# Two selective-scan layers in one kernel: channels regrouped from 128 + 64 into three blocks of 64

## The chip, the cores and the metric

The kernel runs on one core of a Trainium2 chip. The metric is the device time of one execution in microseconds. The kernel before took 1862.71 us (median of 3 runs, 1862.12 to 1892.24). Engine names are those of the profile: PE is TensorE (matmuls, PEld its weight loads), DVE VectorE, ACT ScalarE, POOL GpSimd, SP the engine that here only issues DMAs.

## The reference

Two layers follow each other on an image of 64 x 64 tokens with 96 channels. Each is `x = x + layer(groupnorm(x))`. Cut to what matters (the second layer; the first has raster scans along rows and columns in place of the snake):

```python
xin, z = split(x @ in_proj_w.T)              # 96 -> 192 + 192 channels
xc = silu(depthwise_conv3x3(xin))            # 192 channels
xs = [xc, reversed, snake order, reversed snake]          # 4 directions, 4096 tokens
x_dbl = xs @ x_proj; dts, B, C = x_dbl                     # 6, 16, 16 values a token
dt = softplus(dts @ dt_proj + bias)
h  = h * exp(dt * A) + dt * u * B            # along the tokens, 192 channels x 16 states
y  = sum over states (h * C) + u * D
y  = layernorm(sum of the 4 directions, put back) * silu(z)
out = y @ out_proj_w.T
```

The first layer computes its scan by cumulative sums with a decay in the divisor; past the first tokens of each direction the decay has underflowed and nothing is added.

## The kernel before

**Layout.** Channels lie on the 128 partitions, tokens along the free dimension. Channels 0 to 127 are in `u0` (scan input) and `y0` (result), both [128, 4096]. Channels 128 to 191 are in `ud` [128, 4096], which holds them twice, in the lower and the upper 64 partitions (the copy is made by DMA), and in `y1` [128, 2048], where the two partition halves hold different half-chunks of tokens.

**Stages**, in order, for each of the two layers: `head` (groupnorm, input projection, conv, silu, gate to DRAM), the scans, and `tail` (layernorm, gate, output projection, residual).

- `head(l)` projects in eight steps of 512 tokens, copies the result by ACT into padded images `pad0`, `pad1`, and runs six convolutions `conv(b, c)` of [128, 1024]: nine taps each on DVE (L1011 for the first, L1013 for the others), silu on ACT. `y0 = u0 * D` is made by ACT (L1018) after each conv; `y1 = ud * D` by POOL in `start_y1` (L920 to L923), two instructions of 64 x 2048 at the end.
- Layer 0 scans only in `near_scans`: in each direction the first 192 tokens for the slowest states, fewer for the faster ones (`STAY`), in 8 units. A flag computed from the data says whether that is enough; it is in this input, so the full scan under `tc.If` is not executed, and all full scan tiles are layer 1's.
- Layer 1 runs `scans`: 16 groups (2 orders x 2 directions x 4 chunks of 1024 tokens), each with 24 tiles of [128, 1024]. The first 16 (T=0) are one state of channels 0 to 127; the other 8 (T=1) are two states of channels 128 to 191, one in each partition half. 384 tiles in all.
- `tail(l)` runs eight steps of 512 tokens, in a software pipeline of `centre` (mean by matmul with `pos`, subtraction, square), `scale` (variance by matmul, reciprocal root on ACT, gain and gate on DVE), `project` (output projection, residual add on DVE), and in layer 1 `tokens` (transposes and store).

**One scan tile.** PE spreads a row of B over the partitions into PSUM (L777, weights `sel` or `selh`), ACT makes `m = exp(dt * A)` into PSUM (L792), DVE makes `b = B * du` (L793) and scans `h = m * h + b` (L816), POOL multiplies by a spread row of C (L832; `cb` is loaded from DRAM by one DMA of 512 KB for T=0, two of 256 KB for T=1), and PE adds the tile to `y` in PSUM (L857): for T=0 with the identity, for T=1 with `fold`, which sums the two partition halves and gives 64 rows. The last state of a T is followed by a copy of `y` by ACT (L863). The next T begins with loading `y` back into PSUM by identity matmuls (L854). PSUM holds one `y` [128, 1024], one `B`, and two `m`.

**Order.** The loop over tiles writes the order of the instructions by hand. At tile j it issues the C load of tile j+2, the B matmul and the exp and `b` of j+1, the scan of j, the C product of j-1, and the reduction of j-5 (`LAG`). The prelude of the next group (projection of x to B, C and dt; splitting of B into three bf16 parts, L580; softplus) is cut into steps that are put between the tiles. Softplus is `delta(T)`: ACT L619 to L628 and POOL L629 (`w`), L632 (`ln`), L635 (`dt`) and L638 (`du`), on [128, 1024], once for each T. For the first group, all of it lies ahead of the first `b`.

Queues run in order. SP issues all loads and stores, so a DMA that waits for data holds up those behind it.

The weights of the scans are loaded by `scan_weights`, 26 small DMAs for each layer and order.

Of the kernel before, what the change touches and what calls it, by code (L numbers as in the profile page):

```python
# [16 lines left out]
HW = 64  # L17
L = HW * HW
DM = 96
DI = 192  # L20
NS = 16
RK = 6
TC = 1024
NCH = L // TC
NEAR = 3 * HW


STAY = ((NEAR, 0, 1, 0, 1), (96, 1, 2, 0, 0), (64, 2, 4, 1, 2), (32, 4, NS, 2, NS // 2))
# [7 lines left out]
NV = 16  # L36


@with_exitstack
def two_ss2d_layers(  # L40
# [11 lines left out]
):  # L52

# [31 lines left out]
    make_identity(nc, ident)  # L85
    pos = const.tile([128, 128], F32, name="pos")
    nc.vector.memset(pos, 1.0 / DI)
    fold = const.tile([128, 128], F32, name="fold")
    for h in range(2):
        nc.vector.tensor_add(fold[:, 64 * h : 64 * h + 64], ident[:, 0:64], ident[:, 64:128])  # L90
# [16 lines left out]
    sel = const.tile([NB, 32, 128], BF16, name="sel")  # L107
    nc.vector.tensor_copy(sel, i3.unsqueeze(2).to_broadcast([NB, 32, 128]))
# [8 lines left out]


# [6 lines left out]
    u0 = pers.tile([128, L], F32, name="u0")  # L125
    ud = pers.tile([128, L], F32, name="ud")
    y0 = pers.tile([128, L], F32, name="y0")

    y1 = pers.tile([128, L // 2], F32, name="y1")
    xs = dpool.tile([DM, L], F32, name="xs")  # L130

# [15 lines left out]
    def views(l, p, base, cc):  # L147


        n = base.shape[-1] // NCH  # L150
        if p == 0:
            return [(base[:, cc * n : (cc + 1) * n], lambda s: s)]
        if l == 0:
            v = base.rearrange("p (h w) -> p w h", w=HW)
            k = TC // HW
            return [
                (v[:, cc * k : (cc + 1) * k, :], lambda s: s.rearrange("p (w h) -> p w h", h=HW))
            ]

        k = n // HW // 2  # L160
        v = base.rearrange("p (r two w) -> p r two w", two=2, w=HW)[:, cc * k : (cc + 1) * k]

        def part(o):
            return lambda s: s.rearrange("p (r two w) -> p r two w", two=2, w=HW)[:, :, o, :]

        return [(v[:, :, 0, :], part(0)), (v[:, :, 1, ::-1], part(1))]

    def columns_of_half(base, h, cols):

        half = slice(64 * h, 64 * h + 64)  # L170
        v = base[half].rearrange("p (c r w) -> p w c r", c=NCH, w=HW)[:, cols]

        def part(s):
            return s[half].rearrange("p (w c h r) -> p w c h r", c=NCH, h=2, r=TC // HW // 2)[
                :, :, :, h, :
            ]

        return v, part

    def near_views_y1():  # L180

        k = NEAR // HW
        lo, hi = slice(0, 64), slice(64, 128)
        out = [
            (0, y1[lo, 0:NEAR], lambda s: s[lo]),
            (1, y1[hi, L // 2 - NEAR :][:, ::-1], lambda s: s[hi]),
        ]
        for h in range(2):
            v, part = columns_of_half(y1, h, slice(0, k))
            out.append((2, v, part))  # L190
            v, part = columns_of_half(y1, h, slice(HW - k, HW))

            out.append((3, v, lambda s, part=part: part(s[:, ::-1])))
        return out

    def near_views(base):

        v = base.rearrange("p (h w) -> p w h", w=HW)
        k = NEAR // HW

        def flat(s):
            return s

        def columns(s):
            return s.rearrange("p (w h) -> p w h", h=HW)

        return [
            (base[:, 0:NEAR], flat),
            (base[:, L - NEAR :][:, ::-1], flat),
            (v[:, 0:k, :], columns),  # L210
            (v[:, HW - k :, :][:, ::-1, ::-1], columns),
        ]
# [5 lines left out]
    def scan_weights(l):  # L218

        xw, dwb, am = [], [], []
        for p in range(2):
            lp = 2 * l + p
            w = swp.tile([128, 4, NC], F32, tag=f"xw{p}", name=f"xw{lp}")
            v = swp.tile([128, 4, 128], F32, tag=f"dwb{p}", name=f"dwb{lp}")
            e = swp.tile([128, 4, NS + 1], F32, tag=f"ab{p}", name=f"ab{lp}")
            a = swp.tile([128, 2, 4, NS], F32, tag=f"am{p}", name=f"am{lp}")
            nc.vector.memset(v[96:128], 0.0)
            for d in range(2):  # L230
                r = slice(NB + RK * d, NB + RK * d + RK)
                rr = slice(RK * d, RK * d + RK)
                hi = slice(64 * d, 64 * d + 64)
                c0 = NB + 2 * RK + NS * d
                for q, T in ((d, d), (2 + d, 2)):
                    nc.sync.dma_start(out=w[:, q, 0 : NC - NS], in_=xpw[lp, :, T, 0 : NC - NS])
                    nc.sync.dma_start(
                        out=w[:, q, NC - NS :], in_=xpw[lp, :, T, c0 : c0 + NS]
                    )
                nc.sync.dma_start(out=v[r, d, :], in_=dtw[lp, rr, d, :])  # L240
                nc.sync.dma_start(
                    out=v[NC : NC + 1, d, :],
                    in_=alb[lp, :, d, NS : NS + 1].rearrange("p o -> o p"),
                )
                nc.sync.dma_start(out=e[:, d, :], in_=alb[lp, :, d, :])
                for h in range(2):
                    half = slice(64 * h, 64 * h + 64)
                    nc.sync.dma_start(out=v[r, 2 + d, half], in_=dtw[lp, rr, 2, hi])
                    nc.sync.dma_start(
                        out=v[NC : NC + 1, 2 + d, half],  # L250
                        in_=alb[lp, hi, 2, NS : NS + 1].rearrange("p o -> o p"),
                    )
                    nc.sync.dma_start(out=e[half, 2 + d, :], in_=alb[lp, hi, 2, :])

            nc.scalar.activation(a[:, 0, 0:2], e[:, 0:2, 0:NS], AF.Exp)
            for h in range(2):
                half = slice(64 * h, 64 * h + 64)
                nc.scalar.activation(
                    a[half, 0, 2:4, 0 : NS // 2], e[half, 2:4, h:NS:2], AF.Exp
                )  # L260
            nc.vector.tensor_scalar_mul(a[:, 1, 0:2], a[:, 0, 0:2], -0.5)
            nc.vector.tensor_scalar_mul(
                a[:, 1, 2:4, 0 : NS // 2], a[:, 0, 2:4, 0 : NS // 2], -0.5
            )
            nc.vector.tensor_scalar_mul(a[:, 0, 0:2], a[:, 0, 0:2], -1.0)
            nc.vector.tensor_scalar_mul(
                a[:, 0, 2:4, 0 : NS // 2], a[:, 0, 2:4, 0 : NS // 2], -1.0
            )
            xw.append(w)
            dwb.append(v)  # L270
            am.append(a)
        return xw, dwb, am

    def near_scans(weights):
# [5 lines left out]
        with ExitStack() as sc:  # L280
# [5 lines left out]
            def spare(name):  # L286
                return pps.tile([128, 1024], F32, tag="m", name=name, bufs=2)

            def parts(t):
                return t.rearrange("p (d w) -> p d w", w=NEAR)  # L290
# [3 lines left out]
            us = []  # L294
            for T, u in enumerate((u0, ud)):
                t = once.tile([128, WN], F32, name=f"nus{T}")
                for i, (v, f) in enumerate(near_views(u)):
                    copy = (nc.gpsimd.tensor_copy, nc.vector.tensor_copy, nc.scalar.copy)[i % 3]
                    copy(f(parts(t)[:, i]), v)
                us.append(t)  # L300
            halves = [slice(0, WN // 2), slice(WN // 2, WN)]
            for h, s in enumerate(halves):
                ps = spare(f"npj{h}")[0:NC, 0 : WN // 2]
                nc.tensor.matmul(ps, xw[:, 0, :], us[0][:, s], start=True, stop=False)
                nc.tensor.matmul(ps, xw[0:64, 2, :], us[1][0:64, s], start=False, stop=True)
                (nc.scalar.copy, nc.vector.tensor_copy)[h](xd[0:NC, s], ps)


            C = {}
            for w in sorted({w for w, *_ in STAY}):  # L310
                C[w] = dram.tile([NS, 4 * w], F32, name=f"nC{w}")
                nc.sync.dma_start(
                    out=C[w].rearrange("n (d w) -> n d w", w=w),
                    in_=parts(xd[NC - NS : NC])[:, :, 0:w],
                )

# [10 lines left out]

            dt, du, S = (
                [once.tile([128, WN], F32, name=f"n{nm}{T}") for T in range(2)]
                for nm in ("dt", "du", "S")  # L330
            )

            def delta(T):
                for h, s in enumerate(halves):
                    ps = spare(f"npd{T}{h}")[:, 0 : WN // 2]
                    nc.tensor.matmul(
# [918 lines left out]
```

## Time and profile before

| | us |
|---|---|
| timed runs | 1862.71, 1862.12, 1892.24; median 1862.71 |
| profiled execution | 1858.14 (span 1856.3, mean TensorE clock 0.853) |
| load and groupnorm statistics | 0 to 24 |
| head of layer 0 | 24 to 99 |
| near scans of layer 0 | 99 to 175 |
| tail of layer 0 | 175 to 249 |
| head of layer 1 | 249 to 330 |
| gap before the first `b` | 330 to 363 |
| scans of layer 1 | 363 to 1783 |
| tail of layer 1 | 1783 to 1856 |

The stages are read from the timeline: where the first and the last instruction of each lie. Inside the scans the period of one tile is 3.60 us: `b`, then the scan, on DVE, with small gaps. The data moved are 231.91 MB, mostly C rows spread over the partitions:

```profile
cb<-C SPq DMA_DIRECT2D x256, 512.0 KB, 4.4
cb<-C SPq DMA_DIRECT2D x256, 256.0 KB, 4.1
```

The columns are destination and source, the issuing queue, the number of DMAs, the size of each, and the median time from issue to landing in us.

### The profile page before, as it was taken

What the parts mean: (1) busy time and instruction counts of PE and PEld (TensorE: products, weight loads), DVE (VectorE), ACT (ScalarE), POOL (GpSimd) and SP (SyncE); (2) the same over time, 40 slices, a digit from 0 to 9 for tenths busy, and PEclk for the clock granted to TensorE, in tenths of its full rate; (3) what the DMA queues carried; (4) which work ended last, traced back from release to release, by engine and by line L of the source; (5) the groups of instructions that cost most, each with busy time, mean ns of one, the idle gap of its engine ahead of it and who ended that gap; (6) DMA issues with size and microseconds to landing.
All of it is one profiled execution on the core that took longest, in us unless ns stands there. A gap on an engine that the chain in (4) does not pass through costs nothing.

```text
span 1856.3 us, 12455 instructions
## 1 busy us (share of the span) xinstructions
PE 1416.7 (76%) x3427; PEld 519.5 (28%) x3427; DVE 1626.8 (88%) x1162; ACT 948.8 (51%) x1321; POOL 1262.0 (68%) x569
## 2 busy tenths in 40 slices
PE   6446973487778797978787878787878878797788
PEld 3014220122223232323232323233232323242322
DVE  7975679289999999999999999999999999999956
ACT  3453653445555645555464545555555564645323
POOL 0252003378888878797979797978888888889720
PEclk8555787588898998989898989898989899898969
DMA  4321312134454444445353545444445444544451
GB/s 98 89 57 45 86 43 68 53 131 131 150 148 141 149 142 142 137 147 156 117 171 124 150 141 144 148 133 161 129 148 148 148 145 135 148 142 148 137 135 34
DMA packets 90640, 231.91 MB, mean 125 GB/s; under 512 B 29984, under 2 KB 31440, under 8 KB 90464
## 3 DMA queue, kind: packets, MB, share of 16 engines
q1 hardware_dynamic: 88448, 230.23, 41.2%
q10 hardware_dynamic: 2112, 0.79, 0.2%
q8 instruction: 29, 0.48, 0.1%
q14 instruction: 51, 0.42, 0.1%
HBM read 216.72 MB, written 12.16 MB: 123 GB/s over the span
## 4 chain that ended last, share of the span: by engine, by line
DVE 49%; PE 14%; ACT 11%; POOL 9%; issue 4%; DVEq 1%; POOLq 0%; ACTq 0%
DVE h L816 36%; ACT m L792 9%; DVE b L793 9%; POOL hc L832 4%; PE y L857 4%; DVE acc L1013 3%; PE y L854 2%; PE B L777 2%; POOL w L629 1%; POOL dt L635 1%; POOL du L638 1%; PE v L1088 1%; PE pd L605 1%; DVEq L816 1%; PE m L1077 1%
## 5 line engine op out<-in xcount | busy, mean ns | idle before, releaser
L832 POOL TENSOR_TENSOR hc<-h,cb 128x1024 f32<-128x1024 f32 x384 | 896.6, 2358 | 230.8 <-PE y L857 138.3
L816 DVE TENSOR_TENSOR_SCAN h<-m,carry,b 128x1024 f32<-128x1024 f32 x288 | 676.7, 2350 | 43.6 <-ACT m L792 6.0
L792 ACT ACTIVATE m<-dt,am 128x1024 f32<-128x1024 f32 x384 | 427.8, 1115 | 392.2 <-DVE h L816 374.7
L793 DVE TENSOR_TENSOR b<-B,du 128x1024 f32<-128x1024 f32 x384 | 461.5, 1202 | 62.5 <-POOL du L638 33.3
L857 PE MATMUL y<-hc,ident 128*128 128x512 f32 x1024 | 507.7, 618 | 6.1 <-POOL hc L832 6.1
L777 PE MATMUL B<-B,sel 96*128 96x512 bf16 x512 | 168.0, 412 | 179.4 <-DVE b L793 178.7
L857 PEld LDWEIGHTS y<-hc,ident 128*128 128x128 f32 x1024 | 198.0, 197 | 217.5 <-issue 156.3
L816 DVE TENSOR_TENSOR_SCAN h<-m,b 128x1024 f32<-128x1024 f32 x96 | 219.9, 2290 | 15.4 <-ACT m L792 2.6
L857 PE MATMUL y<-hc,fold 128*64 128x512 f32 x512 | 181.1, 665 | 20.4 <-POOL hc L832 20.4
L826 ACT COPY carry<-h 128x1 f32<-128x1 f32 x288 | 52.9, 184 | 184.4 <-DVE h L816 183.8
L777 PEld LDWEIGHTS <-sel 96*128 96x128 bf16 x512 | 47.2, 100 | 356.4 <-issue 353.7
L777 PE MATMUL B<-B,selh 96*128 96x512 bf16 x256 | 79.1, 391 | 77.9 <-DVE b L793 77.9
L1013 DVE SCALAR_TENSOR_TENSOR acc<-pad,v,acc 128x1024 f32<-128x1024 f32 x96 | 130.3, 1418 | 0.3
L923 POOL TENSOR_SCALAR y<-ud,ds 64x2048 f32<-64x2048 f32 x4 | 38.7, 9671 | 127.2 <-DMA ud<-ud 127.0
L580 PE MATMUL rs<-xd,ident 96*96 96x512 f32 x128 | 69.1, 622 | 33.0 <-issue 32.0
L854 PE MATMUL y<-y,ident 128*128 128x256 f32 (+1 forms) x144 | 87.8, 768 | 6.0 <-ACT y L863 5.8
L629 POOL TENSOR_TENSOR w<-w,t 128x1024 f32<-128x1024 f32 x32 | 75.4, 2355 | 23.7 <-ACT t L628 23.7
L632 POOL TENSOR_TENSOR ln<-ln,w 128x1024 f32<-128x1024 f32 x32 | 75.2, 2349 | 2.4
L635 POOL TENSOR_TENSOR dt<-dt,ln 128x1024 f32<-128x1024 f32 x32 | 75.4, 2357 | 1.4
L857 PEld LDWEIGHTS y<-hc,fold 128*64 128x64 f32 x512 | 40.7, 147 | 126.5 <-issue 64.9
L605 PE MATMUL pd<-xd,dwb 29*128 29x512 f32 x128 | 70.1, 655 | 5.2 <-DVE h L816 5.2
L777 PEld LDWEIGHTS <-selh 96*128 96x128 bf16 x256 | 23.8, 99 | 179.3 <-issue 179.2
(185 smaller groups left out, 1385.3 us busy)
## 6 DMA issues: line engine op xcount, KB each, us to landing
cb<-C SPq DMA_DIRECT2D x256, 512.0 KB, 4.4
cb<-C SPq DMA_DIRECT2D x256, 256.0 KB, 4.1
szd<-sz SPq DMA_DIRECT2D x16, 256.0 KB, 2.2
szt<-szd SPq DMA_DIRECT2D x16, 256.0 KB, 5.3
xT<-xs SPq DMA_DIRECT2D x16, 192.0 KB, 5.4
szd<-sz SPq DMA_DIRECT2D x16, 128.0 KB, 2.2
ud<-ud SPq DMA_DIRECT2D x8, 256.0 KB, 3.1
szt<-szd SPq DMA_DIRECT2D x16, 128.0 KB, 5.7
```

The source lines that it names most:

```text
L605: nc.tensor.matmul(ps[:, s.start - o : s.stop - o], dwb[p][96 : NC + 1, 2 * T + d, :], xd[96 : NC + 1, s], start=True, stop=True,)
L629: nc.gpsimd.tensor_sub(w, w, t)
L632: nc.gpsimd.tensor_add(ln, ln, w)
L635: nc.gpsimd.tensor_add(dt[:, s], dt[:, s], ln)
L777: nc.tensor.matmul(ps[:, s.start - B0 : s.stop - B0], lhs, me["B3"][:, s.start - XB : s.stop - XB], start=True, stop=True,)
L792: nc.scalar.activation(a, me["dt", T], AF.Exp, scale=am[p][:, 0, q, n : n + 1])
L793: nc.vector.tensor_mul(b[:, rest], ps[:, XB - B0 : TC - B0], me["du", T][:, rest])
L816: nc.vector.tensor_tensor_scan(along(d, h), along(d, a), along(d, b), 0.0 if c == first else carry[T][:, n : n + 1], ALU.mult, ALU.add,)
L832: nc.gpsimd.tensor_mul(hc, live.pop(("h", j)), live.pop(("C", j)))
L854: nc.tensor.matmul(to, ident, of, start=(q == 0), stop=False)
L857: nc.tensor.matmul(ps[half] if split else ps[:, s], lhs[:, 0:64] if split else lhs, v[:, s], start=(n == 0 and not l), stop=(n == ns - 1),)
L1013: nc.vector.scalar_tensor_tensor(acc, src, wk, acc, ALU.mult, ALU.add)
```

## The change

All 192 channels become three blocks T = 0, 1, 2 of 64. `u[T]` and `y[T]` are [128, 2048]: the lower 64 partitions hold the first half of each 1024-token chunk, the upper ones the second half (`HALF`, `HT` = 512). Every scan tile is now 64 channels x two states; a group still has 24 tiles (3 blocks x 8 pairs of states) of [128, 1024]. The tile's own instructions on ACT, DVE and POOL keep their sizes.

- *Softplus* runs on [128, 512] for each of three blocks, half the columns; then `both` copies the result by DMA into the two-state layout, four DMAs of 128 KB each for `dt` and for `du`.
- *Reduction*: always `fold` into 64 rows, two column halves into one [128, 512] bank of `y`, two buffers. `y` is loaded back by one or two matmuls.
- *Projection* to B, C and dt: six matmuls over 64 rows at one step instead of two steps.
- *C rows*: always two DMAs of 256 KB.
- *Conv*: over whole padded rows, 2 x 526 contiguous elements instead of 16 x 64; the rows at the edges of the half-chunks come from extra matmuls (`borders`); `start_y` on POOL runs after each conv on 128 x 1024, six times per layer.
- *Near scans*: `u` gathered by PE, softplus once on [128, 1152], doubled by DMA, six units instead of eight.
- *Tail*: four steps of 1024 tokens, last chunk first, `pos` with a block for each half, output projection by six matmuls over 64 rows.
- *Scan weights*: 44 DMAs instead of 26 for each layer and order. The full scan of layer 0, not executed here, becomes a function of its own (`far_scans`).

The core of the diff:

```diff
-STAY = ((NEAR, 0, 1, 0, 1), (96, 1, 2, 0, 0), (64, 2, 4, 1, 2), (32, 4, NS, 2, NS // 2))
+FEWER = ((64, 1, 2), (32, 2, NP))
...
-    u0 = pers.tile([128, L], F32, name="u0")
-    ud = pers.tile([128, L], F32, name="ud")
-    y0 = pers.tile([128, L], F32, name="y0")
-    y1 = pers.tile([128, L // 2], F32, name="y1")
+    u = [pers.tile([128, L // 2], F32, name=f"u{T}") for T in range(3)]
+    y = [pers.tile([128, L // 2], F32, name=f"y{T}") for T in range(3)]
...
 (scans)
+                def project():
+                    ps = spare(f"pj{k}")[0:NC]
+                    for T in range(3):
+                        for h, half in enumerate(HALF):
+                            nc.tensor.matmul(
+                                ps[:, halves[h]], xw[p][half, d, T, :], me["u"][T][half],
+                                start=(T == 0), stop=(T == 2),
+                            )
...
+                    def lost():
+                        nc.gpsimd.tensor_sub(me["w"], me["w"], me["t"])
+                        nc.gpsimd.tensor_add(me["ln"], me["ln"], me["w"])
+                    def whole():
+                        nc.gpsimd.tensor_add(me["sp"], me["sp"], me["ln"])
+                        nc.gpsimd.tensor_mul(me["su"], me["sp"], me["u"][T])
+                    def double():
+                        for nm, of in (("dt", "sp"), ("du", "su")):
+                            t = me[nm, T] = pre.tile([128, TC], F32, tag=f"{nm}{T}", ...)
+                            both(t.rearrange("p (h t) -> p h t", h=2), me[of])
...
+                        (6, 7, 9, 10, 12, 13, 14, 15, 16, 17, 18, 19, 20, 21, 22),
+                        [
+                            copies, project, rows, lambda: residual(0), lambda: residual(1),
+                            *delta(0), *delta(1),
+                        ],
+                return early, list(enumerate(delta(2)))
...
-                    live["y"] = pps.tile([128, TC], F32, tag="y", name=f"y{l}_{j}")
+                    live["y"] = pps.tile([128, HT], F32, tag="y", name=f"ys{j}", bufs=2)
...
+                for h, half in enumerate(HALF):
+                    nc.tensor.matmul(
+                        ps[half], fold[:, 0:64], v[:, halves[h]], start=False, stop=(m == NP - 1)
+                    )
...
 (head)
+            def conv(b, s):
+                W2 = HW + 2
+                room = cw.tile([128, 2, SR, W2], F32, tag="acc", name=f"acc{l}_{b}_{s}")
+                acc = room.rearrange("p c r w -> p c (r w)")[:, :, 0 : SR * W2 - 2]
...
+                start_y(nc.gpsimd.tensor_scalar_mul, ds, b, cut)
+            for b in range(3):
+                project(b, 0)
+                project(b, 1)
+                borders(b)
...
 (tail)
+                for T in range(3):
+                    nc.tensor.matmul(pm, pos, y[T][:, cut], start=(T == 0), stop=(T == 2))
...
+                for T in range(3):
+                    for h, half in enumerate(HALF):
+                        nc.tensor.matmul(
+                            po[:, h], op[half, T, :], gs[T][half], start=(T == 0), stop=(T == 2)
+                        )
```

## The prediction

> **What bounds it now.** I read the busy line first, then the slices, the chain of waits, and the waits of VectorE inside the scan stage.
>
> ```profile
> PE 1416.7 (76%) x3427; PEld 519.5 (28%) x3427; DVE 1626.8 (88%) x1162; ACT 948.8 (51%) x1321; POOL 1262.0 (68%) x569
> ...
> DVE  7975679289999999999999999999999999999956
> ...
> DVE 49%; PE 14%; ACT 11%; POOL 9%; issue 4%; DVEq 1%; POOLq 0%; ACTq 0%
> ```
>
> VectorE (DVE) is at nine tenths from slice 10 to 38 and lower outside. So there are two regimes. The timeline gives these stages, in us from the span's start: load 0-24, head(0) 24-99, near scans 99-175, tail(0) 175-249, head(1) 249-330, a gap of 33 until the first `b`, the scans 363-1783 (1418.6 from first `b` to last scan) and tail(1) to the end. In the scan stage a tile costs one `b` and one scan:
>
> ```profile
> L816 DVE TENSOR_TENSOR_SCAN h<-m,carry,b 128x1024 f32<-128x1024 f32 x288 | 676.7, 2350 | 43.6 <-ACT m L792 6.0
> ...
> L793 DVE TENSOR_TENSOR b<-B,du 128x1024 f32<-128x1024 f32 x384 | 461.5, 1202 | 62.5 <-POOL du L638 33.3
> ...
> L857 PE MATMUL y<-hc,ident 128*128 128x512 f32 x1024 | 507.7, 618 | 6.1 <-POOL hc L832 6.1
> ```
>
> With the small gaps between instructions the timeline shows a cadence of 3.60 us (3.54 where the scan starts from a constant). 288 x 3.60 + 96 x 3.54 = 1377, so about 42 of the 1418.6 are waits. The waits of VectorE between 363 and 1783 name them (sum, number, mean):
>
> ```profile
> DVE b L793 <- PE B L777: 29.0, 36, 4.5
> DVE h L816 <- ACT m L792: 8.6, 11, 1.1
> ```
>
> (29.0 over 36 is 0.8 each; the last column is the largest.) The change keeps 384 tiles of 128x1024, so **the stage can give at most those 42 us**. The rest must come from the stages at both ends, here by windows (length; busy PE, PEld, DVE, ACT, POOL; TensorE clock; DMA share; GB/s):
>
> ```profile
> 24.00:99.00 75.00, 42.68 (x64) 12.41 (x64) 72.36 (x71) 37.42 (x55) 17.23 (x2) 0.64 0.26 65
> 99.00:175.00 76.00, 41.36 (x139) 26.59 (x139) 49.61 (x85) 41.09 (x82) 27.89 (x32) 0.52 0.17 36
> 175.00:249.00 74.00, 65.08 (x98) 17.14 (x98) 45.64 (x75) 40.22 (x48) 0.82 (x8) 0.75 0.36 93
> 249.00:330.00 81.00, 41.48 (x80) 14.18 (x79) 73.35 (x67) 34.52 (x50) 20.77 (x2) 0.73 0.19 52
> ```
>
> The heads are VectorE's (72 of 75, 73 of 81), the tails TensorE's (65 of 74), and near is bound by none.
>
> **What the Trainium skill says.** "SBUF — State Buffer", section "Who interferes with whom": a VectorE instruction with two SBUF inputs and GpSimd exclude each other on a shared port; one SBUF input does not. The trace agrees: a conv tap (L1013, pad and acc from SBUF) takes 1.28 us, but 4.62 and 4.64 us for the two that coincide with L923 on GpSimd; `b` (one input in PSUM) keeps 1.20 us beside `hc`. "TensorEngine Tiling (Array Packing)", section "Key Properties": matmuls in different rows or columns of the array run side by side. The trace agrees for columns: four `fold` records of 64 columns take 1.08 us, four `ident` records 1.9. For rows it shows two chance pairs only (`o` and `m` of the tail near 1810.6, 0.67 and 0.69 us, overlapping). "TensorE: Matmul & The Clock Gate" says an idle TensorE drops to half clock; in the trace 64x512 and 128x512 records cost 1.0 us in the first 24-29 us of a tail and 0.52 later.
>
> **The change, part by part** (estimates; plus is slower).
>
> *Scans.* Per tile: `exp`, `b`, scan and `hc` unchanged. TensorE: `ident` reductions (1.9 us) become `fold` pairs (1.1), so 256 tiles lose 0.8 us of TensorE; B matmuls are the same. The starting value of y is 1 or 2 `ident` matmuls of [128,512] for each T instead of up to 4, and y has two PSUM buffers, so that the next T does not wait for ACT's copy (L863). Those T switches are where B comes late: clock dips to 0.55 and most of the 36 waits lie there. GpSimd: 8 softplus operations of 2.35 us (18.8 per group) become 12 of 128x512. No row of that size is here; half of 2.35 is 1.18, so 14.1, bounds 12 and 18. ACT: 12 softplus activations of 1.1 become 18 of about 0.6 (half the columns above the 0.2 us that a small copy takes), less 2 us per group.
> Added: doubling `dt` and `du` by 8 DMAs of 128 KB for each T and group, 384 in all, 50 MB on 231.9 MB, and 8 x 0.45 = 3.6 us of SP's issue. They wait for GpSimd's `whole`, and queued behind them on SP are the `cb` loads; for these GpSimd's `hc` waits. A `cb` load is issued 10.8 us (three cadences) ahead of its `hc` and lands in 4.4, leaving 6.4; 3.6 of issue leaves 2.8. And `hc` may be late by a tile before the 4 `h` buffers stop VectorE. So I cost it at 0, bound 0 to +1 per burst, 48 in all. `dt(k+1, T)` itself is ready over five cadences ahead for T=0. C is now always two loads of 256 KB, 256 more issues on SP over 1377 us, same bytes: 0.
> What remains of the 42: about 14 (the first tiles, `exp` after a long ACT step). **-28, bounds -38 to +10.**
>
> *Start-up of the scans (33 us).* Six ACT softplus steps of 1.02-1.15 become 0.6 (-3), four GpSimd steps of 2.35 become 1.2 (-4.6), `y0` on ACT goes (-1.1), the doubling DMA adds 8 issues and one landing, 5.5 (`cb` of 256 KB: 4.1). **-4, bounds -8 to +4.**
>
> *Heads.* (a) Conv(0,0) now needs 9 in-projections and border matmuls ahead of it; before, it began 6.3-6.8 us after the first `xn`, behind pairs of 1.02-2.07 us. In-projection is cut from 16 full to 12 pairs of 64 columns, but border copies add 0.21 each: **+3.5** (+1 to +8). (b) A tap runs over 2 x 526 = 1052 elements instead of 1024: 54 taps x 1.2 x 2.7% = +1.7. (c) `ds*u`:
>
> ```profile
> L923 POOL TENSOR_SCALAR y<-ud,ds 64x2048 f32<-64x2048 f32 x4 | 38.7, 9671 | 127.2 <-DMA ud<-ud 127.0
> ```
>
> two of 9.67 us per layer, at the end of the conv become six of 128x1024 (about 4.8 each) after each conv, five of them under taps. Each stretched tap cost 4.63 - 1.28 = 3.35 us, twice: 6.7 per layer. A half as long operation should hold a tap half as long: 5 x 1.7 = 8.5, **+2**. ACT's `y0` goes, off the path. **+7 for each head** (+2 to +13).
>
> *Near.* ACT exp and tanh (24 + 24) and VectorE's three rows (6.4, 6.3, 11.6) come down by a quarter (6 units for 8), but `us` go through TensorE and ACT, softplus runs on the whole 1152 columns once, and 12 doubling DMAs put two landings of 3-4 us in the chain: -5 and +10. **+5** (-3 to +12).
>
> *Tails.* Per 1024 tokens `m` and `v` take 6 records each in place of 8 (block-diagonal `pos`), `o` 12 records of 64 rows that can go as 6 pairs in place of 8. The steady period is TensorE's: 6.27 us per 512 tokens, 2.1 + 2.1 + 2.06. New per 1024: 3.1 + 3.1 + 3.1 = 9.4 to 12.5 without row pairs, before 12.5. With four periods and fewer, longer steps: tail(0) 4 x 3.1 = **-12** (-16 to -2), tail(1), where the token transposes stay, **-10** (-14 to -2).
>
> *Setup:* `sel` cast of 2.3 us goes, `wide`, `fold2` come: **-1.5.**
>
> Sum: -28 - 4 + 14 + 5 - 22 - 1.5 = **-36**. The profiled execution took 1858.1 us (span 1856.3), so 1822; the median of the three runs, 1862.7, is 4.6 above, so 1826.5. I say 1826.
>
> **Rivals.**
> A. *The waits stay* (chance 0.17): VectorE bounds the scan stage by its own work, the waits move to another place (`exp` on ACT, whose queue holds three softplus blocks), and row pairs do not overlap in the tails. Then scans -8, tails -10 and the rest as above (-4, +14, +5, -1.5): -4.5, 1858. For it: 1.20 + 2.35 is untouched. Against it: the waits lie at the T switches, which the change removes.
> B. *Slower: SP's queue becomes the pacer* (0.16). Each doubling waits on SP for GpSimd, and `cb` behind it is late. It decides when the wait plus 3.6 us of issue plus 1 MB of transfer (3.2 us at 310 GB/s, which is 145 GB/s over the share 0.47) exceeds the 6.4 us of lead plus the tile that the `h` buffers hold (3.6), 10.0. If it does by 1.5 us in each of 48 bursts, +72 takes the place of -28: 1926; by 1.0 us, 1902. For it: a wait of one tile (3.6), 3.6 and 3.2 one after another make 10.4. Against: transfers begin while later ones are issued. Likewise the row projection, now in one step (12 records of 0.52): one after another they are 6.3 us before B(j+1) can follow, against 2.4 of cover.
> C. *Better* (0.19): the heads' start and GpSimd's multiplies hide (+2 each in place of +7), near gains its 5, the scan stage 36 of its 42: 1826 - 10 - 8 - 8 = 1800.
> The change does what it says: block sizes are in the code, so no case for that.
>
> **How the numbers follow.** My case (0.48) is 1826, its own range 1812 to 1842 from the parts' bounds, not all of them at one end. Leaving out most of B (over 1870) and the end of C (under 1795) gives 1795 to 1870. About 2% of the median, 1825.5 and 1900, is what a measurement of this kernel can tell from no change. Faster by over 2%: half of mine (0.24) and C (0.19): 0.43. Slower by over 2%: three quarters of B, 0.12. Same: half of mine, A, the rest of B, 0.45.
>
> **What would show it.** Scans: VectorE's waits on B fall under 10 us in sum, the cadence stays 3.60, first `b` to last scan about 1391; B (the rival) would show `hc` waiting for `cb`, and VectorE for `hc`. Tails: `m`, `v`, `o` at some 9.4 us per 1024 tokens, `o` records in overlapping pairs. Heads: conv starts 3.5 us later after `xn`, taps of 1.32 us, five stretched ones per layer. The first `b` comes 29 us after the end of the head's conv. I am wrong first if VectorE's cadence changes, or if the taps beside GpSimd are stretched more than in proportion to its length.

## The result: 16.9% slower, and the profile after

The changed kernel took 2175.23 us (median of 4 runs, 2174.01 to 2176.87) against 1862.41 for the kernel before: ratio 1.169, 95% interval 1.1665 to 1.1711. One of the four runs of before was in a slower state of the chip (1892.24 us) and is left out of the ratio. The busy line and three rows of the slices of the changed kernel's page:

```profile
PE 1418.6 (65%) x3694; PEld 369.2 (17%) x3694; DVE 1605.4 (74%) x1108; ACT 881.7 (41%) x1386; POOL 1266.7 (58%) x647
...
DVE  7845793867676868686868777777777777777795
...
POOL 0741086575656565656657575757575657574760
PEclk8556866757585858585767776766767676767558
```

VectorE's busy time is about the same as before (1605 for 1627 us) but it is spread over a span 319 us longer: no engine works more than 5 us longer, all wait more. The loss lies in slices 8 to 38. By the timeline, in us:

| stage | before | after | change | forecast |
|---|---|---|---|---|
| head of layer 0, to the end of its conv | 99 | 101 | +2 | +7, setup -1.5 |
| near scans | 75 | 94 | +19 | +5 |
| tail of layer 0 | 74 | 50 | -24 | -12 |
| head of layer 1 | 81 | 79 | -2 | +7 |
| gap, from the head's last tap to the first `b` | 34 | 33 | -1 | -4 |
| scans, first `b` to last scan | 1418.6 | 1766.8 | +348 | -28 |
| tail of layer 1 | 73 | 51 | -22 | -10 |

Outside the scans the change gains some 29 us (408.2 for 437.7; the rows are rounded), where the forecast had 8.5. The whole loss is in the scans. VectorE's waits there, beside the 29.0 and 8.6 us of before (sum, number of times, longest):

```profile
DVE h L815 <- POOL hc L824: 285.8, 76, 7.9
DVE b L806 <- PE B L793: 87.7, 91, 2.6
```

The scan waits for an `h` buffer, which GpSimd's (POOL's) `hc` frees. Why is `hc` late? POOL's own waits in the same stage:

```profile
POOL w L751 <- ACT t L748: 427.4, 46, 11.6
POOL hc L824 <- DVE h L815: 181.9, 109, 3.4
POOL hc L824 <- DMA cb<-C: 22.6, 17, 2.4
```

POOL is 58% busy and yet late: 427 us, 9.3 at a time, go into one instruction, the softplus subtraction `w`, which waits for ACT's last activation `t`. Waiting for C rows (`cb`) cost POOL only 22.6 us. One such place in the timeline of the changed kernel (start, length, engine and line, operation, tiles; in brackets the idle time before and who ended it), first POOL, then ACT:

```profile
1078.77 2.35 POOL L824 TENSOR_TENSOR hc<-h,cb 128x1024 f32<-128x1024 f32 x1 [3.26 <-DVE h L815]
1092.72 1.27 POOL L751 TENSOR_TENSOR w<-w,t 128x512 f32<-128x512 f32 x1 [11.60 <-ACT t L748]
1094.07 1.26 POOL L752 TENSOR_TENSOR ln<-ln,w 128x512 f32<-128x512 f32 x1
1095.42 1.26 POOL L755 TENSOR_TENSOR sp<-sp,ln 128x512 f32<-128x512 f32 x1
1096.76 1.26 POOL L756 TENSOR_TENSOR su<-sp,u 128x512 f32<-128x512 f32 x1
1097.97 9.27 POOL L824 TENSOR_TENSOR hc<-h,cb 128x1024 f32<-128x1024 f32 x4
```

```profile
1086.72 1.12 ACT L802 ACTIVATE m<-dt,am 128x1024 f32<-128x1024 f32 x1
...
1087.85 0.64 ACT L745 ACTIVATE w<-w 128x512 f32<-128x512 f32 x1
1088.38 1.11 ACT L802 ACTIVATE m<-dt,am 128x1024 f32<-128x1024 f32 x1
...
1090.03 0.71 ACT L747 ACTIVATE t<-w,one 128x512 f32<-128x512 f32 x1
...
1090.88 1.12 ACT L802 ACTIVATE m<-dt,am 128x1024 f32<-128x1024 f32 x1
1091.94 0.70 ACT L748 ACTIVATE t<-t,less 128x512 f32<-128x512 f32 x1
```

POOL stands still from 1081.1 to 1092.7 with three finished scans behind `w`, then does four `hc` in a row. ACT cannot reach `t` sooner: in its queue three `exp` (`m`) and carries stand before it, and those wait for the scans. The two queues disagree on where softplus belongs.

This order is not the one written in the loop. A planner orders each engine's instructions when the program is built. The disagreement can be counted in the built program: the number of `exp` that ACT issues before a `t`, less the number of `hc` that POOL issues before the `w` that reads it.

| kernel | lead at each softplus, in tiles |
|---|---|
| before | 1 |
| after | 5, 5, 6 |

(The first group, whose softplus lies ahead of the scans, is left out; the traces show the same leads.) With a lead of 1, `w` falls into its place: in the kernel before, it does not wait at all past the first group. In the changed kernel a `w` waits 9.4 us on average at a lead of 5 and 9.7 at 6. The waits are not in proportion to the lead; what a smaller lead costs, the experiments show.

### The profile page after: what moved, and what is told of

Same layout as the page of the kernel before. It is cut to its first block, busy times and chain, and to the rows that moved or that the text cites. A ratio compares the mean times of both kernels' runs of the same rounds, so it can differ in the third digit from the quotient of the medians.

```text
span 2175.0 us, 14719 instructions
## 1 busy us (share of the span) xinstructions
PE 1418.6 (65%) x3694; PEld 369.2 (17%) x3694; DVE 1605.4 (74%) x1108; ACT 881.7 (41%) x1386; POOL 1266.7 (58%) x647
## 5 line engine op out<-in xcount | busy, mean ns | idle before, releaser
L840 PE MATMUL ys<-hc,fold 128*64 128x512 f32 x1536 | 637.8, 871 | 205.5 <-POOL hc L824 204.7
L793 PE MATMUL B<-B,selh 96*128 96x512 bf16 x768 | 318.2, 508 | 311.2 <-DVE b L806 310.6
L751 POOL TENSOR_TENSOR w<-w,t 128x512 f32<-128x512 f32 x48 | 60.8, 1267 | 435.3 <-ACT t L748 435.3
L840 PEld LDWEIGHTS ys<-hc,fold 128*64 128x64 f32 x1536 | 109.4, 176 | 501.4 <-POOL hc L824 316.0
L883 POOL TENSOR_SCALAR y<-u,ds 128x1024 f32<-128x1024 f32 x12 | 98.8, 8246 | 86.7 <-ACT u L981 86.7
L979 DVE SCALAR_TENSOR_TENSOR acc<-pad,v,acc 128x1052 f32<-128x1052 f32 x96 | 121.8, 1334 | 0.3
L835 PE MATMUL ys<-y,ident 128*128 128x256 f32 (+1 forms) x144 | 87.6, 717 | 50.1 <-POOL y L883 37.8
L724 PE MATMUL pd<-xd,dwb 29*64 29x512 f32 x192 | 69.9, 815 | 18.2 <-ACT B L715 12.3
L752 POOL TENSOR_TENSOR ln<-ln,w 128x512 f32<-128x512 f32 x48 | 60.7, 1264 | 3.7
L755 POOL TENSOR_TENSOR sp<-sp,ln 128x512 f32<-128x512 f32 x48 | 60.7, 1266 | 1.3
```

Of the source, the lines that this page charges most:

```text
L724: nc.tensor.matmul(ps[half], dwb[p][96 : NC + 1, d, T, half], xd[96 : NC + 1, halves[h]], start=True, stop=True,)
L751: nc.gpsimd.tensor_sub(me["w"], me["w"], me["t"])
L793: nc.tensor.matmul(ps[:, s], pick(GROUPS[k][1], m), state[k]["B3"][:, s], start=True, stop=True)
L835: nc.tensor.matmul(f(live["y"]), ident, view, start=(q == 0), stop=False)
L840: nc.tensor.matmul(ps[half], fold[:, 0:64], v[:, halves[h]], start=False, stop=(m == NP - 1))
L883: mul(y[T][:, s], u[T][:, s], ds[:, T : T + 1])
```

## The experiments

Three theories. ORDER: POOL's queue is held by `w`. DOUBLING: the copies of `dt` and `du` hold up SP and the loads. CLOCK: TensorE, at a mean clock of 0.69 in place of 0.85, makes B late. (Line numbers of the edited kernels are up to five above those of the changed one.)

**POOL in the written order.**

```diff
+            sc.enter_context(tc.manual_schedule(engines={mybir.EngineType.Pool}))
             load_exp_ln()
```

> Edit: inside the scans of layer 1 GpSimd (POOL) issues its instructions in the written order; the other engines keep the planner's. Count of leads (exps that ACT issues ahead of the softplus' last activation t, less the hc products that POOL issues ahead of the subtraction w that reads t): 5 to 6 in the changed kernel, 1 in the kernel before, 1 to 3 here. Theory ORDER (POOL's queue is held by w, issued three to four tiles too early): POOL's wait on t falls from 435 us to about 48 x 1 tile x 3.6 = 170 or less, DVE's wait on hc from 286 to under 60, time 1850 to 1930. Theory DOUBLING (the 384 copies on SP and their 50 MB delay cb or du): the order of POOL changes nothing of it, time over 2100. Theory CLOCK (TensorE at 0.69 makes B late): over 2100.

1881.23 us (1880.59 to 1881.87; ratio 1.010 to before). One engine's order takes back 294 of the 313 us. VectorE's wait on `hc` is gone from the list; POOL's waits (sum, number, longest) show 62 us on `t`:

```profile
POOL hc L825 <- DVE h L816: 236.1, 148, 3.9
POOL w L752 <- ACT t L749: 61.9, 31, 4.5
```

ORDER holds: in the scans POOL issues only softplus and `hc`, so the place of softplus is all that this changes there by itself. But the clock stayed at 0.74, and VectorE still waits 82 us for B.

**POOL and ACT in the written order; all engines in it** (the same line with more engines, or none named).

> Edit: in the scans POOL and ACT both issue in the written order; lead 1 at every softplus, as in the kernel before. Theory ORDER: POOL's wait on t under 50 us, DVE's wait on hc under 20, first b to last scan about 1400, time 1830 to 1850; the TensorE clock returns to about 0.85 without being touched. Theory DOUBLING or CLOCK: over 2100.

1903.03 us, 22 more, although the lead is 1 everywhere: a miss. The written order puts four activations of softplus between two `exp`; VectorE waits 54 us for `exp` (18 in pool_written), and POOL still 110 for `t`.

> Edit: in the scans all engines and SP issue in the written order. Theory ORDER: within 20 us of the run with POOL and ACT in the written order, 1820 to 1860, since only those two queues were wrong. Theory DOUBLING: over 2100, or longer still, since the copies then sit on SP exactly between the cb loads.

1934.90 us, also a miss. VectorE's wait on B is 158 us. So the written order isn't good as such. The part of it that was needed is POOL's, the place of softplus.

Nor is a lead of 1 what counts. Over all the runs here, leads of 4 to 6 (the changed kernel, no_doubling, after_zero) go with 203 to 286 us of VectorE's waits on `hc`; with leads of 1 to 3 (all the others, the kernel before among them) VectorE waits on POOL for 1.1 us at most after the first `b`. A `w` with a lead of 3 does wait, 3.6 us on average in pool_written, but that stays on POOL. That the four `h` buffers take it up fits, and is not shown by a run of its own.

**Without the doubling**, in the changed kernel and with POOL in the written order.

```diff
                     def double():
+                        if k:
+                            me["dt", T], me["du", T] = state[0]["dt", T], state[0]["du", T]
+                            return
                         for nm, of in (("dt", "sp"), ("du", "su")):
```

> Edit: the copies of dt and du into the two-state layout are made for the first group only and used for all groups, so the result is that of other dt and du; softplus and everything else still run. 360 of 384 copies and 47 MB are gone. Theory ORDER: POOL's wait on t stays at some 400 us, time 2100 to 2180. Theory DOUBLING: 1840 to 1900.

2058.63 us: between the two theories. The planner answers to the missing copies with other orders (leads 5, 5, 4 in place of 5, 5, 6), so the run changes two things, and its 117 us can't be divided between them.

> Edit: POOL in the written order, and dt and du doubled by DMA in the first group only and used in all groups, so the result is that of other dt and du. If the doubling is hidden, as the prediction has it: 1870 to 1885, within 10 us of pool_written. If the copies hold up cb or B: 1830 to 1860.

1861.59 us (1855.45 to 1871.91), 20 below pool_written. At this point the doubling seemed to cost something. (The leads changed here too, from 3, 2, 1 to 2, 2, 2.)

**One zero matmul per tile.** In pool_written the TensorE timeline shows the same records at two speeds:

```profile
904.27 0.59 PE L794 MATMUL B<-B,selh 96*128 96x512 bf16 x2 [0.93 <-DVE b L807]
904.79 1.08 PE L841 MATMUL ys<-hc,fold 128*64 128x512 f32 x4
907.85 0.59 PE L794 MATMUL B<-B,selh 96*128 96x512 bf16 x2 [1.98 <-DVE b L807]
...
915.37 1.01 PE L794 MATMUL B<-B,selh 96*128 96x512 bf16 x2 [1.32 <-DVE b L807]
916.32 1.98 PE L841 MATMUL ys<-hc,fold 128*64 128x512 f32 x4
```

After gaps of 1 to 2 us per tile, B takes 1.01 for 0.59 us and the four records of a tile's `fold` pair 1.98 for 1.08: about half clock (granted 0.51 from 915 to 934 us). The edit, on top of POOL's written order, adds work that changes nothing in the result:

```diff
                 ps = live["y"]
+                nc.tensor.matmul(ps, zero, v[:, halves[0]], start=False, stop=False)
                 for h, half in enumerate(HALF):
```

> Edit: POOL in the written order as in pool_written (1881 us), and one extra matmul per tile with a weight matrix of zeros, added into the same y, so the result is unchanged and TensorE has about 0.95 us more work per tile. Theory IDLE CLOCK (the new fold reductions leave TensorE idle for some 2 us per tile, its clock is halved, and B comes late): the clock between 400 and 1780 us rises from 0.76 to 0.88 or more, VectorE's wait on B falls from 82 us to under 45, time 1835 to 1855. Theory LOAD (B is late because TensorE has too much queued at the prelude's steps): the wait on B grows to 100 or more, time 1890 to 1920.

1849.37 us (1847.13 to 1853.68), 32 less than pool_written; ratio to before 0.9932 [0.9924, 0.9939]. More work on TensorE made it faster. One window of pool_written, then the same one of pool_zero (length; busy PE, PEld, DVE, ACT, POOL; clock; DMA share; GB/s):

```profile
800.00:1000.00 200.00, 154.12 (x402) 34.18 (x401) 180.98 (x105) 101.02 (x164) 156.71 (x82) 0.75 0.74 175
```

```profile
800.00:1000.00 200.00, 167.08 (x517) 49.97 (x518) 185.66 (x108) 101.80 (x163) 160.44 (x83) 0.98 0.76 180
```

VectorE's waits on B in the two runs (sum, number, longest):

```profile
DVE b L807 <- PE B L794: 82.4, 93, 2.6
```

```profile
DVE b L809 <- PE B L796: 56.3, 49, 2.1
```

The clock rises from 0.75 to 0.98. VectorE's wait on B fell to 56, not below 45. IDLE CLOCK holds for the clock and the time; the planner's orders may have moved with the added matmul, which ys_first_no_zero below settles.

> Edit: the changed kernel with the planner's order on all engines, and only the zero matmul added. Leads of ACT over POOL 4 to 6, nearly as in the changed kernel (5 to 6). Theory ORDER FIRST (POOL's stall is most of the loss, the clock a smaller part of its own): the clock rises to 0.85 or more, time 2080 to 2160. Theory CLOCK FIRST (the half clock makes POOL's stall): 1850 to 1950.

2126.02 us, with the clock in the scans at 0.88 to 0.91: 49 of the 313 us come back while POOL's leads stay high (4, 5, 6). ORDER comes first.

**The weights of layer 1 later** (a try at the near scans).

```diff
+                i = nc.scalar.activation(a[half, 0], e[half, :, :, h:NS:2], AF.Exp)
+                if l:
+                    tc.keep_in_program_order(i)
...
-        sw = scan_weights(l)
+        sw = None if l else scan_weights(l)
         head(l, xT, w)
+        sw = sw or scan_weights(l)
```

> Edit: POOL in the written order, and layer 1's scan weights are loaded and their exponentials issued on ACT after the head of layer 1, so that they stand in no queue during the near scans. Theory WEIGHTS (the near scans are longer by some 18 us mainly because ACT and VectorE wait 11 us for these loads): near falls from 94 to about 83, time 1868 to 1873. Theory CHAIN (the near scans' length is their own chain, doubling DMAs and TensorE at half clock): near 90 to 94, time 1877 to 1885.

1878.32 us (1875.69 to 1882.76), 3 less: CHAIN, not WEIGHTS. VectorE waits as long in the same place (11.6 us for 11.0), now for ACT's copy of the projection.

> Edit: both of these on top of the written order on POOL. If IDLE CLOCK and WEIGHTS hold, their gains add: 1825 to 1845, below the kernel before. If only one holds: 1845 to 1870.

1848.66 us (1846.60 to 1852.08): no gain on pool_zero.

**VectorE too in the written order.**

> Edit: as pool_zero (POOL in the written order, one zero matmul per tile; 1849 us), and VectorE too issues in the written order. On VectorE the planner has put two scans and then two b one after another at 30 places in the changed kernel and in pool_zero, at 15 in pool_no_doubling, at none in layer 1 of the kernel before, and here at one. There is one B buffer, so the second b of such a pair must wait for its B. Theory SWAP (these pairs are the rest of VectorE's waits on B): the wait falls from 56 us to under 25, time 1820 to 1838. Theory COPIES (the 20 us that pool_no_doubling gained are the DMAs' own): 1845 to 1855.

1853.09 us (1849.65 to 1853.98): SWAP falls. The wait on B is 75 us. But the same without the doubling:

> Edit: as pool_dve_zero, and dt and du doubled in the first group only and used in all, so the result is that of other dt and du. Theory SWAP: within 6 us of pool_dve_zero. Theory COPIES: 15 to 25 us below it.

1825.68 us, 27 less. With ACT in the written order as well:

> Edit: as pool_dve_zero, with ACT in the written order too, which puts four activations of softplus between two exps. From pool_act_written, where that cost 22 us against pool_written (VectorE's wait on exp 54 us for 18): 1840 to 1860, slower than pool_dve_zero.

1898.64 us, dearer still than forecast, as in pool_act_written.

The trace of pool_dve_zero shows what the 27 us can be. In 14 of the 16 groups VectorE waits once for 2 to 4.9 us for B, each time behind the projection `pj`: 44 of the 75 us. TensorE, then VectorE:

```profile
1191.29 0.59 PE L796 MATMUL B<-B,selh 96*128 96x512 bf16 x2 [1.13 <-DVE b L809]
1193.54 5.48 PE L690 MATMUL pj<-us,xw 64*124 64x512 f32 x12 [1.67 <-DVE h L818]
1198.96 1.35 PE L842 MATMUL ys<-hc,zero 128*128 128x512 f32 x2
1200.24 1.08 PE L844 MATMUL ys<-hc,fold 128*64 128x512 f32 x4
1201.25 0.60 PE L796 MATMUL B<-B,selh 96*128 96x512 bf16 x2
```

```profile
1194.72 2.34 DVE L818 TENSOR_TENSOR_SCAN h<-m,carry,b 128x1024 f32<-128x1024 f32 x1
1201.90 1.23 DVE L809 TENSOR_TENSOR b<-B,du 128x1024 f32<-128x1024 f32 x1 [4.83 <-PE B L796]
```

`pj` stands directly behind B, waits for a scan to free its PSUM buffer, here drops to half clock (granted 0.50 from 1193 to 1199 us; 5.48 us for 2.84 at full clock), and the next B queues behind it and behind a reduction that had long been ready. Without copies the planner had put `pj` between two reductions, where it doesn't wait. So I fixed TensorE's order as well and moved the reduction ahead of the step:

```diff
                     (stage_B, j + 1),
+                    (stage_r, j - LAG),
                     (None, j),
                     (stage_a, j + 1),
                     (stage_s, j),
                     (stage_c, j - 1),
-                    (stage_r, j - LAG),
```

> Edit: as pool_dve_zero (1853 us), with TensorE too in the written order, and that order changed: the reduction of tile j-5 is written ahead of the prelude's step, so that it lies between B and the projection. In pool_dve_zero the projection stands directly behind B, waits 1.67 us for its PSUM buffer, and the next b waits 2 to 4.9 us for its B once per group. Theory PLACE (this place costs some 16 x 2 to 3 us): those waits go, VectorE's wait on B falls from 75 us to under 45, time 1815 to 1830. Theory COPIES (the doubling's DMAs cost it): 1845 to 1855.

**1783.90 us (1782.38 to 1785.41), ratio to before 0.9584, interval 0.957 to 0.9597: 4.2% faster than the kernel before and 18% faster than the changed one.** POOL, VectorE and TensorE are in this order, and the zero matmul stays. PLACE holds in its sign: the wait on B is far under 45 us, the time below its range. But the run fixes TensorE's whole order and moves the reduction, and no run does one alone on pool_dve_zero. (all_written had TensorE in the written order with the reduction in its old place, but ACT and SP in the written order too and no zero matmul; there VectorE waited 158 us for B.) The gain, 69 us on pool_dve_zero, is about twice what was expected. VectorE's waits from 350 us on:

```profile
DVE b L809 <- DMA du<-su: 26.3, 1, 26.3
DVE y L1031 <- PE m L1029: 11.1, 2, 10.5
DVE b L809 <- PE B L796: 3.7, 10, 1.1
```

The wait on B fell from 75 us to 3.7, since the short waits (0.4 to 1.1 us) at the other steps went with the long ones. First `b` to last scan is 1378 us (352.2 to 1730.0), what 384 cadences come to. The slices of its page:

```profile
DVE  7956569399999999999999999999999999999986
...
PEclk8655787589999999999999999999999999999999
```

> Edit: as ys_first, with dt and du doubled in the first group only and used in all, so the result is that of other dt and du; the orders of TensorE, VectorE and POOL are the same. Theory PLACE: within 8 us of ys_first. Theory COPIES: 20 us or more below it.

1784.63 us (1784.31 to 1785.45), 0.7 more. With the orders of these three engines held (ACT and SP keep the planner's), leaving out 47 MB of copies changes nothing. POOL waits 40.6 us for `cb` with them and 2.2 without, but VectorE doesn't wait for POOL in either. What the runs without copies gained on pool_written and pool_dve_zero was therefore, most likely, the planner's order.

> Edit: as ys_first without the zero matmuls. Theory IDLE CLOCK: the clock in the scans falls back to about 0.75, 20 to 40 us above ys_first (pool_written against pool_zero: 32). If the order alone keeps B early at half clock: within 8 us of ys_first.

1820.48 us (1819.13 to 1820.92), 36.6 above ys_first, the clock in the scans, from 400 to 1600 us, at 0.75 to 0.77 again; here the orders are held, and VectorE waits 37.5 us for B where ys_first has 3.7. A window of ys_first, then the same one of ys_first_no_zero (columns as above):

```profile
400.00:600.00 200.00, 165.54 (x543) 51.80 (x542) 193.53 (x113) 110.26 (x179) 162.22 (x83) 1.00 0.74 175
```

```profile
400.00:600.00 200.00, 156.11 (x422) 34.45 (x421) 188.88 (x109) 102.84 (x168) 157.19 (x82) 0.75 0.71 169
```

This order without added work is 2.2% faster than before.

## Why the prediction was wrong

**The step that failed** is in *Scans*: "GpSimd: 8 softplus operations of 2.35 us (18.8 per group) become 12 of 128x512 ... 14.1". The busy time was right (12 x 1.265 = 15.2), but I let shorter work mean less delay, and gave it no wait. An instruction that stands four to five tiles too early in a queue costs what it waits, 9.3 us, not what it runs, 1.27. By way of `hc` and the `h` buffers that became 286 us of VectorE's waits, and pool_written, which mends this order alone, took 294 us back. The bound of "+10" had no room for it. I did not ask whether the orders of two engines fit together, which the count of leads would have shown (1 before, 5 to 6 after). Of the rivals, B named the sign and the last link (`hc` late, `h` buffers exhausted, VectorE held), but not the cause: `cb` cost POOL 22.6 us, and with the order held the doubling costs nothing. I priced the doubling's copies at 0; with the order held, that was right. Neither of the two signs that I named first for being wrong came: VectorE's cadence stayed, and the taps beside POOL were not stretched more than in proportion to its length. (One sum is off: in rival C near goes from +5 to -5, which is 10, not 8; nothing hangs on it.)

**A second step**, "256 tiles lose 0.8 us of TensorE", was counted as relief. TensorE's work fell, its clock fell with it, and B came no earlier. The prediction cites the Trainium skill ("TensorE: Matmul & The Clock Gate") for an idle TensorE at half clock, and applied it to the tails only. In the scans this costs 32 to 37 us, by pool_zero against pool_written and by ys_first_no_zero against ys_first.

**A third:** the projection, "12 records of 0.52", stood in rival B alone, as "one after another they are 6.3 us before B(j+1) can follow". They do not run one after another: 12 records take 2.84 us at full clock. But the projection waits for a PSUM buffer between B and the reduction, and VectorE waited 44 us behind it in pool_dve_zero; with the mended order, which also moved the rest of TensorE's work, ys_first gave back 69.

**Right:** the cadence stayed 3.60 us; the stage could give 42 us at most, and in ys_first it gave 41. The tails were forecast at half of what they gave. Per 1024 tokens I had 9.4 us of `m`, `v` and `o`; the steady part of tail(1) shows 8.3, the records of `o` in row pairs (TensorE's timeline of the changed kernel):

```profile
2149.39 2.74 PE L1035 MATMUL v<-sq,pos 128*128 128x512 f32 x6
2152.06 2.82 PE L1053 MATMUL o<-g,op 64*96 64x512 f32 x12
```

That makes 4 x (12.5 - 8.3) = 17 of the 24 and 22 us. Part of the rest lies at the start of the tails: before, TensorE's granted clock was 0.50 from 175 to 205 and from 1783 to 1810 us, and in the changed kernel the records of tail(1) have their full-speed length some 7 us after the first `m`. The prediction named these first "24-29 us" and put no saving on them; what shortened them no run tells.

**Heads:** +2 and -2 for +7 each. Conv(0,0) began 32.4 us after the start (29.75 before), +2.6 for +3.5. The five stretched taps per layer didn't come: three in all took 2.05 to 2.09 us, the others 1.31, and POOL's `start_y` was stretched in their place, as POOL's timeline of the changed kernel shows:

```profile
281.13 56.98 POOL L883 TENSOR_SCALAR y<-u,ds 128x1024 f32<-128x1024 f32 x6 [36.62 <-ACT u L981]
```

Six took 57 us, where I had 4.8 each; their line's longest is 42.3, its shortest 2.8. The 9.67 us that I halved was itself a mean of 12.0, 5.9, 14.9 and 5.9: beside taps, POOL's multiply had been stretched before too. (The trace of before has four stretched taps, two per layer, of 4.62 to 4.63 us.) TensorE's first load of y waits 38 us for them, ACT 3, VectorE not.

**Gap:** -1 for -4; the first `b` came 33 us after the head's last tap, where I had 29.

**Near:** +19 for +5. VectorE's timeline of the changed kernel shows where: 11 us of waiting until the projection is there (its copy starts at 115.9 us, before the change at 107.4), and the doublings:

```profile
115.25 0.19 DVE L220 TENSOR_SCALAR am<-am 128x48 f32<-128x48 f32 x1 [10.97 <-ACT am L219]
...
143.61 0.34 DVE L372 TENSOR_TENSOR top<-nS,most 128x12 f32<-128x12 f32 x3 [8.80 <-DMA nS<-nsums]
...
149.27 2.15 DVE L441 TENSOR_TENSOR nnb<-nB,ndu 128x768 f32<-128x768 f32 x3 [4.17 <-DMA ndu<-ndus]
```

The first wait is put down to the weights' exponential; pool_late_weights took that away, and the wait stayed. The gather of `u` on TensorE, at half clock (0.52 in this stage, as before), and the doubling are what is left; no run has shown how much each costs.

Not settled: why the planner moved softplus forward on POOL. The runs show what its order costs, not what it took for its estimate.

## What to carry to other kernels

- When a change touches a planned order, count on each pair of engines how far the consumer's queue runs ahead of the producer's. Here leads of 1 to 3 tiles cost VectorE nothing and leads of 4 to 6 cost it 203 to 286 us. A busy share of 58% on an engine that others wait for can mean that its queue is blocked; look at what it waits for.
- Before you thank a change for taking work off TensorE, look at the gaps it leaves per tile: TensorE's reductions became shorter here, its clock fell, and filling the gaps with a matmul of zeros gained 32 to 37 us.
- An experiment that removes instructions may also reorder the rest. Hold the order of the engines, then remove; leaving out the doubling "gained" 20, 27 and 117 us before that, and nothing after.

## What the hardware showed that I had not expected

- TensorE fell to half clock without any long gap, with about one short one per tile of 3.6 us, and its clock stayed near 0.75 on average. In ys_first_no_zero no gap between its matmuls from 400 to 1700 us is longer than 2.0 us (in pool_written some reach 3.0). A matmul against a matrix of zeros, 0.95 to 1.02 us per tile, held the clock at 0.97 to 1.00; the longest gap in ys_first is 1.5 us. The Trainium skill ("TensorE: Matmul & The Clock Gate", section "Why this matters for your kernels") warns of gaps above some 3 us; here repeated shorter ones were enough.
- Twelve matmul records over 64 rows took 2.82 to 2.84 us, six of `v` over 128 rows 2.74: row halves run side by side. The records of `o` start in pairs, 6 to 7 ns apart.
- Beside VectorE's taps, POOL's multiply of 128x1024 took up to 42 us (2.8 undisturbed) and no tap took over 2.1; before the change one of 64x2048 took up to 14.9 us (5.9 undisturbed), and two taps per layer took 4.6. Why POOL now loses most of it no run tells.
